# Where the weights of six head pairs are staged in an attention and feed-forward kernel

## The chip, the core and the metric

The kernel runs on one core of one Trainium2 chip. A core has TensorE (PE: matmuls, with PEld for the loads of its stationary operand), VectorE (DVE), ScalarE (ACT), GpSimd (POOL) and SyncE (SP, which here issues nearly all DMAs). The metric is the time of one execution on the device, in microseconds (us): 3020.89 us is the median of three runs of the kernel before, which ranged from 3020.09 to 3022.32 us. Everything is float32. The first dimension of an on-chip tile is the 128 partitions; a tile of `[128, 1024]` float32 takes 4 KB of each partition.

## What is computed

One transformer block over 2048 rows of 1024 columns. Cut to what matters:

```python
q, k, v = (layernorm(x) @ W for W in (Wq, Wk, Wv))     # 16 heads of 64 columns
q, k = rotary(q), rotary(k)
attn = softmax(causal(q @ k.T) / sqrt(64)) @ v          # per head
x = x + layernorm(attn @ Wo)
Wg, Wu, Wd = dequant_nf4(...)                           # 16-value codes times block scales
x = x + layernorm((silu(layernorm(x) @ Wg.T) * (layernorm(x) @ Wu.T)) @ Wd.T)
```

## The kernel before

**Numbers in two parts.** A float32 operand of a matmul is split in a high part (a cast to the type fp32r, on ACT) and a low part (the rest, a subtraction on DVE or POOL). A product is then three matmuls (`mm3`, lines 110 to 115): high by high, high by low, low by high.

**Stages.** The 16 heads are worked on in eight pairs `m = 0..7`, since two heads of 64 columns fill 128 columns of a weight. For a pair, `prep_qkv` (line 221) prepares three weights by `prep_w` (line 174): the 1024 x 128 columns of Wq, Wk and Wv. Then `qkv(m, c)` (line 224) makes the three products for each of four row groups `c` of 512 rows; it applies the rotary table `tab`, splits the results and stores them to DRAM (`qs`, `ks`, `vs`). Attention (`scores`, `weighted`) reads them back by head.

The q, k and v of pairs 0 and 1 are made at the start. Those of pairs 2 to 7 are made beside the attention: while the attention of one pair runs, three or four `(m, c)` groups of later pairs are interleaved with it (lines 384 to 418; `pace` ties each product to a score matmul, so that they spread over 85% of the pair). Line 394 asks for a new pair's weights when the attention of a pair starts; where the new pair begins within an attention pair, `group` (line 379) asks for them. Then follow the output projection, the dequantized gate and up matmuls, and the down projection.

**Preparing a weight.** `prep_w` takes a 4 KB room `wf`, loads 512 KB into it from DRAM on SP's queue (line 177), and makes the two parts in an 8 KB room `w`: two casts on ACT (line 184) and, for pairs from the third on (`m > 1`), two subtractions on DVE (line 186). There are 18 such loads for `m > 1`, three to a pair.

**Rooms.** All SBUF tiles come from tags with a fixed number of rooms:

```python
SLOTS = {"hd": (7, 8), "w": (3, 8), "xc": (4, 8), "pa": (6, 8), "pb": (2, 4), "f4": (4, 4), "pw": (3, 4), "t2": (3, 2), "ol": (1, 2)}
```

The first number is the count of rooms, the second the KB of each. The rooms of a tag are handed out in the order in which the program asks for them, and a load waits until the room it is given is free. During the attention `f4` (four rooms) serves, for each `(m, c)` group, the table `tab`, the split q and k (`hl`, one each) and the split v (`vo`): four requests to a group. In the kernel before it also serves `wf`. `pb` (two rooms) holds the weight Wv of pair 1 in two halves at the start (`prep_qkv(1, ("pa", "pa", "pb"))`, line 346; `prep_w` makes two tiles of four blocks for this tag); it is asked for again only after the attention, for the rows of the output projection (line 504). The `w` tag has three rooms, one for each weight of the pair in work: a new weight can be cast when the last product with the old one in its room is done.

**Order.** The order of each engine's instructions is fixed when the program is built: a planner takes them by the program's order as their priority and by a modelled time line (`schedule_with_timeline_sim=True`, line 830), in which an instruction is placed when its operands and its room are there. At run time each engine goes through its list in order and waits at semaphores. DMAs issued on SP are a list of that kind too.

Of the kernel before, what the change touches and what calls it, by code (L numbers as in the profile page):

```python
# [10 lines left out]
F32 = mybir.dt.float32  # L11
# [13 lines left out]
P = 128  # L25
KE = E // P
# [31 lines left out]
def block_kernel(ctx, tc, x, wq, wk, wv, wo, gu_codes, gu_scales, d_codes, d_scales, cos_sin, out):  # L58
# [15 lines left out]
    def slot(tag, shape, dtype, name):  # L74
        assert int(np.prod(shape[1:])) * 4 <= SLOTS[tag][1] * 1024, (tag, shape)
        return sb.tile(shape, dtype, tag=tag, name=name, bufs=SLOTS[tag][0])
# [25 lines left out]
    def f32(ap):  # L102
        return ap.bitcast(F32)
# [69 lines left out]

    def prep_w(w, m, scale, tag="w"):

        wf = slot("f4", [P, KE, P], F32, "wf")
        load(wf, w[:, m * P : (m + 1) * P].rearrange("(k p) n -> p k n", p=P))
        n = KE // 2 if tag == "pb" else KE
        parts = []
        for k0 in range(0, KE, n):  # L180
            t = slot(tag, [P, 2, n, P], FR, "w")
            for k in range(0, n, STEP):
                src, hi, lo = wf[:, k0 + k : k0 + k + STEP], t[:, 0, k : k + STEP], t[:, 1, k : k + STEP]
                A.activation(hi, src, AF.Copy, scale=scale)  # L184
                if m > 1:
                    V.scalar_tensor_tensor(lo, src, scale, f32(hi), ALU.mult, ALU.subtract)
                else:
                    if scale != 1.0:
                        G.tensor_scalar(src, src, scale, 0.0, ALU.mult, ALU.add)
                    G.tensor_tensor(lo, src, f32(hi), ALU.subtract)  # L190
            parts += [t[:, :, k, :] for k in range(n)]
        return parts
# [28 lines left out]
    def prep_qkv(m, tags=("w", "w", "w")):  # L221
        return [prep_w(w, m, sc, tag) for w, sc, tag in zip((wq, wk, wv), (0.125, 1.0, 1.0), tags)]
# [207 lines left out]
    m = KE - 1  # L430
# [403 lines left out]
```

## Time and profile before

| | us |
|---|---|
| median of three runs | 3020.89 |
| the profiled execution | 3012.18 |
| its span in the profile | 3010.4 |
| PE busy | 2912.1 |
| DVE busy | 2032.5 |
| ACT busy | 1697.9 |
| POOL busy | 954.8 |

The span is the time between the first and the last instruction of the profiled execution; 1.8 us of its time lie outside it. Busy is the time in which an engine had an instruction in work. The granted clock (PEclk) is the share of full speed that TensorE was given; over the whole span it is 0.992. DMA share is the mean busy share of the core's 16 DMA engines. The attention lies roughly between 165 and 1490 us.

### The profile page before, as it was taken

The numbers are of one execution on the slowest core, as the hardware profiler recorded it, in microseconds if no ns is written. First come the engines' busy times: TensorE is split into PE (matmuls) and PEld (weight loads), VectorE is DVE, ScalarE is ACT, GpSimd is POOL, SyncE is SP. The second block draws the span as 40 slices with busy tenths as digits, with TensorE's granted clock in tenths as the row PEclk, the third lists the DMA queues.
The fourth block names the chain that finished last, engine by engine and source line by source line (L and its number), as shares of the span: only waits on it lengthen the run. The fifth ranks groups of instructions, "written<-read, shape, count | busy, mean of one in ns | idle before, by whom it ended". The sixth has DMA issues, their size and how long they took to land.

```text
span 3010.4 us, 42538 instructions
## 1 busy us (share of the span) xinstructions
PE 2912.1 (97%) x14168; PEld 2406.1 (80%) x14168; DVE 2032.5 (68%) x4171; ACT 1697.9 (56%) x3569; POOL 954.8 (32%) x1055
## 2 busy tenths in 40 slices
PE   7989999999998999999999999999999999999998
PEld 6868888787877787777787888888888888888886
DVE  6567778787867677777666667776666677444347
ACT  4256667776766666676565555655555566333234
POOL 5344344443444343454332121222221223100034
PEclk9999999999999999999999999999999999999999
DMA  8787665657557558472356344434434444744446
GB/s 295 271 255 233 213 214 186 213 171 226 157 196 195 172 176 254 139 229 90 123 178 230 109 138 139 154 129 140 135 121 135 139 151 151 255 140 144 150 144 234
DMA packets 271740, 536.01 MB, mean 178 GB/s; under 512 B 22944, under 2 KB 113056, under 8 KB 255648
## 3 DMA queue, kind: packets, MB, share of 16 engines
q1 hardware_dynamic: 269344, 529.10, 54.3%
q10 hardware_dynamic: 2176, 4.19, 0.4%
q8 instruction: 112, 1.84, 0.3%
q14 instruction: 108, 0.88, 0.1%
HBM read 371.98 MB, written 161.22 MB: 177 GB/s over the span
## 4 chain that ended last, share of the span: by engine, by line
PE 79%; DMA 9%; DVE 5%; ACT 2%; issue 1%; POOL 1%; SPq 1%; POOLq 0%; ACTq 0%; DVEq 0%
PE bk L112 14%; PE bk L114 14%; PE bk L113 14%; PE pt L315 6%; PE qkv L112 4%; PE qkv L114 4%; PE qkv L113 4%; PE o L320 3%; PE o L319 3%; PE s L273 3%; PE s L275 3%; PE pj L466 2%; PE pj L464 2%; PE pj L465 2%; DMA wf<-in_wq 2%
## 5 line engine op out<-in xcount | busy, mean ns | idle before, releaser
L305 POOL TENSOR_SCALAR prob<-prob,rc 128x512 f32<-128x512 f32 (+3 forms) x640 | 404.9, 659 | 440.1 <-DVE rc L300 231.0
L112 PE MATMUL bk<-x,wt 128*128 128x512 f32 x1376 | 534.1, 390 | 4.6 <-ACT x L118 3.7
L113 PE MATMUL bk<-x,wt 128*128 128x512 f32 x1376 | 535.9, 389 | 0.0
L114 PE MATMUL bk<-x,wt 128*128 128x512 f32 x1376 | 535.7, 389 | 0.0
L283 ACT ACTIVATE prob<-s,mxs 128x512 f32<-128x512 f32 (+3 forms) x640 | 402.6, 633 | 145.9 <-DVE mxs L281 88.7
L119 DVE TENSOR_TENSOR pw<-pt,pw 128x512 fp32r<-128x512 f32 (+3 forms) x640 | 378.4, 601 | 119.7 <-ACT pw L118 117.9
L529 ACT ACTIVATE ln<-cs,bias 128x512 f32<-128x512 f32 x520 | 359.8, 716 | 107.0 <-DVE mb L535 20.4
L118 ACT CAST pw<-pt 128x512 fp32r<-128x512 f32 (+3 forms) x640 | 324.1, 527 | 169.6 <-PE pt L315 137.0
L315 PE MATMUL pt<-ident,prob 128*128 128x128 f32 x2176 | 345.4, 275 | 7.3 <-DVE pw L119 6.0
L315 PEld LDWEIGHTS pt<-ident,prob 128*128 128x128 f32 x2176 | 267.6, 141 | 62.0 <-issue 7.7
L112 PEld LDWEIGHTS bk<-x,wt 128*128 128x128 f32 x1376 | 258.4, 188 | 59.1 <-ACT x L118 3.9
L114 PEld LDWEIGHTS bk<-x,wt 128*128 128x128 f32 x1376 | 258.7, 188 | 53.9
L113 PEld LDWEIGHTS bk<-x,wt 128*128 128x128 f32 x1376 | 258.8, 188 | 53.5
L281 DVE TENSOR_REDUCE mxs<-s 128x1 f32<-128x512 f32 x384 | 260.9, 681 | 58.6 <-PE s L275 57.3
L273 PE MATMUL s<-k,q 128*128 128x512 f32 (+3 forms) x640 | 265.0, 415 | 23.9 <-ACT prob L283 19.7
L320 PE MATMUL o<-pw,v 128*128 128x512 f32 (+3 forms) x640 | 247.0, 388 | 8.3 <-DVE pw L119 7.6
L319 PE MATMUL o<-pw,v 128*128 128x512 f32 (+3 forms) x640 | 243.8, 381 | 8.6 <-ACT pw L118 6.7
L112 PE MATMUL qkv<-xc,w 128*128 128x512 f32 x576 | 230.9, 401 | 11.8 <-ACT w L184 6.3
L113 PE MATMUL bk<-bt,at 128*128 128x512 f32 x616 | 239.6, 389 | 0.0
L114 PE MATMUL bk<-bt,at 128*128 128x512 f32 x616 | 238.8, 389 | 0.0
L112 PE MATMUL bk<-bt,at 128*128 128x512 f32 x616 | 238.6, 389 | 0.0
L275 PE MATMUL s<-k,q 128*128 128x512 f32 (+3 forms) x640 | 235.6, 371 | 0.0
(150 smaller groups left out, 5504.7 us busy)
## 6 DMA issues: line engine op xcount, KB each, us to landing
xc<-xd SPq DMA_DIRECT2D x96, 1024.0 KB, 9.1
q<-qs SPq DMA_DIRECT2D x128, 256.0 KB, 6.8
ast<-S SPq DMA_DIRECT2D x44, 512.0 KB, 3.7
cs<-in_gu_scales SPq DMA_DIRECT2D x172, 128.0 KB, 3.2
cs<-in_gu_codes SPq DMA_DIRECT2D x86, 256.0 KB, 3.0
A<-in SPq DMA_DIRECT2D x66, 256.0 KB, 2.1
S<-in SPq DMA_DIRECT2D x66, 256.0 KB, 3.1
ast<-A SPq DMA_DIRECT2D x33, 512.0 KB, 4.5
```

Source lines behind the costliest of these rows:

```text
L112: r = T.matmul(o, lhsT=w[:, 0], rhs=xx[:, 0], start=first, stop=False)
L113: T.matmul(o, lhsT=w[:, 0], rhs=xx[:, 1], start=False, stop=False)
L114: T.matmul(o, lhsT=w[:, 1], rhs=xx[:, 0], start=False, stop=last)
L119: return V.tensor_tensor(lo, src, f32(hi), ALU.subtract)
L273: mm = T.matmul(s, lhsT=q[:, 0, j * P : (j + 1) * P], rhs=k[:, b:e], start=True, stop=False)
L275: T.matmul(s, lhsT=q[:, 1, j * P : (j + 1) * P], rhs=k[:, b:e], start=False, stop=True)
L283: A.activation(prob[i][:, j, : e - b], s, AF.Exp, bias=mx, scale=sign, accum_out=sums[:, j % BATCH, i : i + 1])
L305: G.tensor_scalar(p, p, rc[:, jj % BATCH, i : i + 1], 0.0, ALU.mult, ALU.add)
L315: T.transpose(pt[:, j * P : (j + 1) * P], prob[kb // 4][:, j, kb % 4 * P : (kb % 4 + 1) * P], ident)
L319: T.matmul(o[:, cs], lhsT=v[:, kb, :], rhs=pw[:, 0, cs], start=kb == 0, stop=False)
L320: T.matmul(o[:, cs], lhsT=v[:, kb, :], rhs=pw[:, 1, cs], start=False, stop=kb == nk - 1)
L529: A.activation(ln, c8, AF.Prelu, bias=bias_of[ab], scale=ab[0], alpha=ab[2])
```

## The change

One line. The staging room of a weight is taken from `pb` for pairs from the third on (`m > 1`), and from `f4` as before for the first two.

```diff
     def prep_w(w, m, scale, tag="w"):
 
-        wf = slot("f4", [P, KE, P], F32, "wf")
+        wf = slot("pb" if m > 1 else "f4", [P, KE, P], F32, "wf")
         load(wf, w[:, m * P : (m + 1) * P].rearrange("(k p) n -> p k n", p=P))
```

No load, cast, subtraction or matmul is added or taken away. The 18 weights of `m > 1` now share two rooms that nothing else uses during the attention, and the four rooms of `f4` serve `tab`, `hl` and `vo` alone.

## The prediction

> **What bounds the kernel now.** I began with the page. TensorE is busy for all but 98 us of the span, so whatever this change brings has to come out of those 98 us, or out of matmuls that ran at a lower clock.
>
> ```profile
> span 3010.4 us, 42538 instructions
> ...
> PE 2912.1 (97%) x14168; PEld 2406.1 (80%) x14168; DVE 2032.5 (68%) x4171; ACT 1697.9 (56%) x3569; POOL 954.8 (32%) x1055
> ```
>
> Next I asked for everything that touches the tile wf, from 300 us on, where the weights of pairs 3 to 7 are prepared (m = 2 comes earlier). The rows give each load's time in SP's queue (ns, min/median/max), who waited for the loads, and their time to landing.
>
> ```profile
> L177 SPq DMA_DIRECT2D wf<-in_wv x5: 1065/3812/10472, 353.8 to 1147.6; - x5
> ...
>   ACT w L184: 14.1, 6
> ...
> DMA to landing us min/median/max: 6.0/12.3/16.2
> ```
>
> A load lands 12.3 us after its issue, and ACT's list has the cast in it sooner than that: ACT stood still for 14.1 us at six casts. The loads start at 340, 535, 730, 931 and 1145 us. So I cut out the stretch around each (busy us and counts of PE, PEld, DVE, ACT and POOL, then granted clock, DMA share, GB/s):
>
> ```profile
> 336.00:362.00 26.00, 24.70 (x141) 20.28 (x139) 21.74 (x52) 21.10 (x56) 5.47 (x10) 1.00 1.00 332
> 527.00:556.00 29.00, 26.04 (x129) 20.08 (x128) 23.85 (x66) 20.79 (x55) 11.04 (x16) 0.88 0.88 251
> 728.00:752.00 24.00, 21.82 (x115) 16.91 (x114) 18.25 (x47) 17.52 (x45) 5.97 (x10) 1.00 1.02 299
> 930.00:964.00 34.00, 27.53 (x146) 21.34 (x145) 27.78 (x77) 25.95 (x70) 11.80 (x19) 0.95 1.02 286
> 1137.00:1166.00 29.00, 24.73 (x127) 20.39 (x126) 21.48 (x58) 19.58 (x52) 5.65 (x11) 0.88 1.03 285
> ```
>
> and the long stretches between them:
>
> ```profile
> 362.00:527.00 165.00, 163.26 (x901) 136.93 (x899) 127.82 (x325) 113.25 (x296) 77.43 (x104) 1.00 0.58 191
> 556.00:728.00 172.00, 167.64 (x929) 140.91 (x928) 131.18 (x336) 116.46 (x310) 76.33 (x102) 1.00 0.57 181
> 752.00:930.00 178.00, 171.75 (x940) 142.63 (x939) 134.38 (x352) 119.16 (x321) 78.65 (x108) 1.00 0.51 162
> 964.00:1137.00 173.00, 168.36 (x909) 139.66 (x909) 125.08 (x324) 110.86 (x292) 73.91 (x102) 0.99 0.56 179
> ```
>
> In the five windows PE is idle for 142 - 124.8 = 17.2 us (12%), between them for 688 - 671.0 = 17.0 us (2.5%). The DMA engines are full in the windows and half used between them. And three windows have a lower clock.
>
> The waits of the last window show the path, from the load to ACT, to DVE and to PE:
>
> ```profile
> ACT w L184 <- DMA wf<-in_wq: 4.8, 1, 4.8
> ...
> DVE w L186 <- ACT w L184: 4.1, 1, 4.1
> PE qkv L112 <- ACT w L184: 3.9, 1, 3.9
> ```
>
> Two finer stretches price the clock that follows:
>
> ```profile
> 946.80:950.20 3.40, 3.40 (x12) 2.56 (x11) 2.42 (x8) 1.99 (x6) 0.26 (x1) 0.51 1.16 241
> ...
> 1155.00:1162.00 7.00, 5.35 (x14) 4.27 (x15) 4.86 (x10) 6.03 (x15) 2.17 (x4) 0.51 1.00 287
> ```
>
> **The change, part by part.** Nothing is added or removed; what moves is when the 18 loads may be issued.
>
> *Why they are late now.* In f4 the three requests of a new pair come after tab, hl, hl and vo of the previous group, so a load starts only when that group is nearly over: the third pair's first load, at 185.02, was released by POOL's rotary addition (L251), the last reader of that group's tab. In pb a load has only older weights before it. The rooms alternate: q of pair m+1 takes the room of k of pair m, k that of v; v takes the room of its own q. So q and k of the next pair can be issued as soon as this pair's k and v are cast, most of a pair earlier (190 us lie between windows), and v as soon as its q is cast. With the load there, a cast waits only for its w room, so q, k and v are cast one by one behind the last group's three products. At m = 3 those products ended at 314, 327 and 336, against casts at 356 to 361 now: v's load would get some 20 us, more than the longest landing (16.2).
>
> *What the waits cost PE.* By the waits of the windows: m = 3, 0.2 (qkv behind the cast); m = 4, nothing (its 2.1 us gap at 538 follows ACT's wait for a store of at); m = 5, 1.3 + 0.5 (the second, a pw cast queued behind on ACT); m = 6, 2.6 + 1.4 (pw and prob behind two waiting casts) + 1.4 (scores waiting for q<-qs, issued at 953.6, behind weight loads in SP's list and in full DMA engines); m = 7, 3.9. Sum 11.3 us.
>
> *The clock.* PE worked 3.40 us at 0.51 after the gap at m = 6 and 5.35 us at 0.51 around that of m = 7. At full clock it would have saved 3.40 x 0.49 + 5.35 x 0.49 = 1.7 + 2.6 = 4.3 us.
>
> The trace has the half clock after gaps of at most 2.6 us at m = 6. [...]
>
> *What is late next.* 11.3 + 4.3 = 15.6 us would go if nothing else waited. But 11.3 is only two thirds of the windows' 17.2 us of idle: the rest ends on prob, pw and q, and would still do so. I credit two thirds: 15.6 x 2/3 = 10.4 us. Bounds: nothing at all, up to windows as quiet as their neighbours (17.2 - 0.025 x 142 = 13.7) with all three half-clock stretches gone (4.3 + 3.0 for the 5.96 us of PE work between 537 and 544), 21.0 us.
>
> *The third pair.* Its pb rooms are held by pair 1's Wv until the last product of (1, 3) ends at 178.3; q's load then starts about 7 us earlier than now, but in front of the four 1 MB loads of xc (178 to 181). Gain: at most the 0.9 us for which PE waits there. Loss: 1 MB at that window's 314 GB/s is 3.3 us, and a half-clock step like that of 168 to 175 (6.83 us long) 3.4 more. I take zero, nearest to the 0.9.
>
> *Edits at no cost.* f4 now serves four requests per group with four rooms, so each kind gets its own last room back; tab for the next group waits for the rotary of the last, a group (30 us or more) before it is used. The casts moved forward cost ACT 1.2 and DVE 1.4 us each; ACT is 66%, DVE 75% busy between the windows, and that room hides them. If it were not there, three pairs of casts would cost up to 4 us a pair.
>
> *The added wait.* v's load waits on SP for the subtraction (L186) of its q. Behind it on SP stand at and vs stores, tab, and the loads of v and q that the next scores need. It is free if SP comes to it after the cast. Its price otherwise is a rival below.
>
> *The plan itself.* A changed room reorders all that follows. The stretches between windows run from 1.1% idle (362 to 527) to 3.5% (752 to 930); all 688 us at either end would be 9.6 us less or 7.0 us more. I take zero.
>
> [...]
>
> **Forecast.** The profiled execution (3010.4 span + 1.8) lies 8.7 us under the median; I carry the difference over to the median: 3020.9 - 10.4 = 3010.5 us. Its own range is 3000 (21.0 off) to 3015.
>
> **Rivals.** *Same, 3021:* the stalls only move, because the loads are planned little earlier, or because the order of the rest eats the gain (a loss of 7.0, above). For it: DVE and ACT limit these stretches too. Against: 12% of idle here, 2.5% beside.
>
> *Slower, 3029:* SP reaches v's load before DVE has cast q, and is held with the scores' q loads behind it. The price per hold, from m = 6, is 1.4 us of PE wait and 1.7 us of half clock, 3.1; six holds cost 18.6, less 10.4 is +8.2. Beyond three holds it eats the gain. For it: SP's waits for DVE's hl average 7.6 us (213.7 in 28). Against: those 20 us of slack.
>
> **How the numbers follow.** Forecast 0.6, same 0.2, slower 0.2. The range, 3000 to 3029, runs from the far end of the forecast to the slower case and leaves out about 0.17. 0.2% is 6 us, about what a measurement of this kernel can tell from no change; faster by more takes the forecast's 0.6, within it 0.2, slower 0.2.
>
> **What would show it.** Right: wf loads of q and k tens of us before their casts; ACT's 14.1 us behind wf nearly gone; no half clock near m = 6 and 7; PE busy down about 4 us; SP's new wait behind L186 short. Wrong: loads still within 15 us of their casts, casts waiting for v, or new gaps behind q<-qs.

## The result, and the profile after

The changed kernel takes 3040.13 us (median of five runs, 3037.76 to 3043.68) against 3020.89, a ratio of 1.0069 (95% interval 1.0054 to 1.0083). It is slower by about 21 us, where I forecast a gain of 10.4. Its profiled execution is the median one, while that of the kernel before lay 8.7 us below its median: the two spans are 27.9 us apart, the two medians 19.2. The page of the changed kernel:

```profile
span 3038.3 us, 42520 instructions
...
PE 2927.1 (96%) x14168; PEld 2417.4 (80%) x14168; DVE 2035.4 (67%) x4171; ACT 1695.3 (56%) x3569; POOL 958.8 (32%) x1055
```

PE has the same 14168 matmuls and is busy 15.0 us longer with them: within the span its clock was halved for 86.4 us instead of 49.7. The other 12.9 us of the span are more idle time.

Yet the loads moved as described. The tile wf of the changed kernel from 300 us on (loads in SP's queue, who waited, landing):

```profile
L177 SPq DMA_DIRECT2D wf<-in_wv x5: 373/384/392, 327.8 to 1147.5; - x5
L177 SPq DMA_DIRECT2D wf<-in_wq x4: 378/380/498, 343.2 to 953.5; - x4
...
  DVE w L186: 1.5, 2
...
DMA to landing us min/median/max: 3.6/3.9/16.6
```

No cast of ACT waits for a load any more (14.1 us before), and the median load lands in 3.9 us instead of 12.3: eight of the 13 were issued into idle DMA engines (a DMA share of 0.00 to 0.01 in the 2 us before the issue) and landed in 3.6 to 4.0 us, the other five, issued into full ones (0.97 to 1.07), in 8.2 to 16.6. The same five windows, and below them the four stretches between them (busy us and counts by engine, granted clock, DMA share, GB/s):

```profile
336.00:362.00 26.00, 25.65 (x147) 21.48 (x145) 21.18 (x51) 18.87 (x48) 9.95 (x12) 1.00 0.99 310
527.00:556.00 29.00, 26.02 (x128) 20.88 (x128) 21.68 (x61) 19.21 (x56) 9.00 (x13) 0.94 0.72 227
728.00:752.00 24.00, 22.27 (x109) 17.69 (x108) 16.17 (x37) 14.57 (x37) 9.82 (x13) 0.93 0.38 128
930.00:964.00 34.00, 30.80 (x164) 24.70 (x163) 28.39 (x68) 24.43 (x65) 16.85 (x20) 1.00 0.38 128
1137.00:1166.00 29.00, 29.00 (x160) 24.51 (x159) 23.26 (x55) 20.18 (x52) 11.61 (x16) 1.00 0.46 143
```

```profile
362.00:527.00 165.00, 157.08 (x853) 130.82 (x853) 124.32 (x315) 110.00 (x289) 69.47 (x95) 0.99 0.59 186
556.00:728.00 172.00, 162.91 (x882) 133.73 (x881) 127.05 (x329) 111.71 (x297) 72.52 (x104) 0.99 0.61 181
752.00:930.00 178.00, 171.41 (x938) 141.74 (x937) 131.21 (x348) 118.16 (x318) 72.99 (x103) 0.99 0.59 188
964.00:1137.00 173.00, 161.41 (x867) 133.27 (x867) 123.42 (x332) 110.60 (x299) 68.68 (x99) 0.97 0.64 200
```

In the windows PE's idle time fell from 17.2 to 142 - 133.7 = 8.3 us, and the DMA share of the last three from 1.0 to 0.4. Between them it rose from 17.0 to 688 - 652.8 = 35.2 us. The windows are fixed in time, though, while the changed kernel runs up to 30 us later, so they no longer hold the same work; the next count is free of that.

**Where it was lost.** I gave every matmul the median spacing that its kind has in the trace of before, and read when each kernel had done the same amount of matmul work. The kernel before has done 300 us of it at 341.0, 700 us at 769.0 and 1500 us at 1641.6. The changed kernel is 7.8 us late at the first of these marks, 25.1 at the second, 26.5 at the third. So 7.8 us go by the end of the attention of pair 0, nearly all of them in its first 35 us ("start"), 17.3 in the attention of pairs 1, 2 and most of 3 ("middle"), and only 1.4 in the rest, where the windows of m = 6 and 7 lie.

Cut by the same count, the work of the five windows takes the changed kernel 130.4 us instead of 142, and that of the four stretches between them 715.0 instead of 688. The gain of the windows was there, 11.6 us, and more than twice as much was lost between them.

### The profile page after: what moved, and what is told of

Its sections match the earlier page's. It is cut to its first block, busy times and chain, and to the rows that moved or that the text cites. A ratio compares the mean times of both kernels' runs of the same rounds, so it can differ in the third digit from the quotient of the medians.

```text
span 3038.3 us, 42520 instructions
## 1 busy us (share of the span) xinstructions
PE 2927.1 (96%) x14168; PEld 2417.4 (80%) x14168; DVE 2035.4 (67%) x4171; ACT 1695.3 (56%) x3569; POOL 958.8 (32%) x1055
## 4 chain that ended last, share of the span: by engine, by line
PE 79%; DMA 10%; DVE 5%; ACT 3%; issue 2%; POOL 1%; SPq 0%; POOLq 0%; ACTq 0%; DVEq 0%
PE bk L112 14%; PE bk L113 14%; PE bk L114 14%; PE pt L315 5%; PE qkv L112 5%; PE qkv L113 4%; PE qkv L114 4%; PE o L320 3%; PE s L273 3%; DMA xc<-xd 3%; PE o L319 3%; PE s L275 3%; PE pj L464 2%; PE pj L466 2%; PE pj L465 2%
## 5 line engine op out<-in xcount | busy, mean ns | idle before, releaser
L273 PE MATMUL s<-k,q 128*128 128x512 f32 (+3 forms) x640 | 266.7, 418 | 36.3 <-ACT prob L283 27.9
```

Source lines behind the costliest of these rows:

```text
L273: mm = T.matmul(s, lhsT=q[:, 0, j * P : (j + 1) * P], rhs=k[:, b:e], start=True, stop=False)
```

## The experiments

The first reading of the traces gave these theories. START: the third pair's loads, now ahead of x and k, cost the start. HOLD: SP, waiting for L186 with v's load, holds what stands behind it. PLAN: the planner's new order happens to be a worse one. EARLY WORK and EARLY LOADS: what comes earlier (casts and products, or transfers) stands in the way. OL: the single `ol` room, whose store to `at` lands late. All ratios are to the kernel before, on the same chip; where an expectation gives a time, it counts from the 3020.9 us of the kernel before, or from b_x1's 3011 where it says so. The table has each kernel's ratio and, from its one profiled execution, its extra time against the kernel before in the three stretches. One execution is a small sample (on one chip the kernel before took 3010.8 to 3025.2 us), so a few us in one cell say little. The table also has the time at which ACT issued the load of the rotary table `tab` of group (1, 3), with which the start's loss turns out to go.

| kernel | ratio (95%) | tab issued at | start | middle | rest |
|---|---|---|---|---|---|
| before | 1 | 167.6 | 0 | 0 | 0 |
| the change | 1.0069 (1.0054 to 1.0083) | 172.4 | +7.8 | +17.3 | +1.4 |
| from4 | 1.0095 (1.0079 to 1.0112) | 172.4 | +7.5 | +18.6 | +2.6 |
| only3 | 1.0028 (1.0018 to 1.0039) | 172.5 | +10.0 | +2.9 | -4.6 |
| tied | 1.0048 (1.0032 to 1.0063) | 166.6 | -0.3 | +21.7 | -2.1 |
| hold | 0.9997 (0.9986 to 1.0007) | 168.1 | +0.3 | 0.0 | +1.5 |
| late | 1.0034 (1.0022 to 1.0046) | 168.2 | -0.1 | +16.5 | -2.0 |
| b86 | 0.9987 (0.9974 to 1.0000) | 167.1 | -0.8 | +1.2 | +4.2 |
| a86 | 1.0080 (1.0065 to 1.0095) | 173.3 | +7.4 | +15.6 | +3.2 |
| b_x1 | 0.9986 (0.9976 to 0.9995) | 168.2 | +0.3 | +1.1 | -4.3 |
| a_x1 | 1.0012 (1.0003 to 1.0020) | 172.4 | +7.1 | +7.9 | -5.4 |
| from4_x1 | 1.0000 (0.9990 to 1.0010) | 171.7 | +6.7 | +2.1 | -7.1 |
| startheld | 1.0060 (1.0044 to 1.0076) | 168.5 | +2.9 | +19.4 | +2.8 |
| startheld_x1 | 0.9984 (0.9974 to 0.9993) | 167.1 | +1.8 | +5.6 | -3.9 |
| b_off | 1.0023 (1.0012 to 1.0033) | 168.9 | +0.7 | +2.4 | +6.8 |
| from4_off | 1.0031 (1.0019 to 1.0042) | 173.6 | +9.4 | +3.5 | +2.1 |
| a_off | 1.0037 (1.0024 to 1.0050) | 173.3 | +8.0 | +4.1 | -1.9 |
| startheld_off | 1.0024 (1.0014 to 1.0035) | 168.8 | +3.4 | +6.1 | +1.9 |

### The parts of the change

**from4** and **only3** do the change for the pairs from the fourth on, and for the third alone.

```diff
-        wf = slot("pb" if m > 1 else "f4", [P, KE, P], F32, "wf")
+        wf = slot("pb" if m > 2 else "f4", [P, KE, P], F32, "wf")     # from4
+        wf = slot("pb" if m == 2 else "f4", [P, KE, P], F32, "wf")    # only3
```

> The change for pairs from the fourth on (m > 2); the third pair (m = 2) stages its weights in f4 as before. Theory START (the third pair's casts stand in ACT's list too early and block the first scores, about 7 us): 3033. Theory HOLD (the loads' new wait for the subtraction L186 holds SP's list, 76.5 us in total, and late q, at and xc behind it cost PE): most holds remain, so 3034 to 3040. Theory PLAN (any reordering of this program loses, whatever is moved): anywhere from 3020 to 3045, with no link to the place.

> The change for the third pair alone (m == 2). START: 3028, with ACT's wait of 5 us and more on wf near 180 us. HOLD: 3021 to 3024, since only the third pair's third load waits. PLAN: anywhere from 3020 to 3045.

only3 loses 0.28%, as START forecast (3028, or 1.0024), and by its trace all of it at the start. from4 was meant to leave the start alone and didn't: with the third pair in f4, it is the fourth pair's first loads that find pb empty, and its trace has loads of wf at 174.0 and 174.9, ahead of x, as the change has at 172.4 and 175.6. So from4 has both losses; it says nothing against START.

**tied** is from4 with the loads held in SP's list until their cast is near.

```diff
+        ld = load(wf, ...)
+        if m > 2:
+            after(ld, stored["k", m - 1, 3] if w is wv else stored["v", m - 1, 1])   # the SP stores of ks and vs
```

> The change from the fourth pair on, with each load placed in SP's list behind a store that is issued long after the cast it waits for: q and k of pair m behind the v store of group (m - 1, 1), v behind the k store of (m - 1, 3). The loads are still early enough, and SP's wait for L186 should be gone. HOLD with START: 3009 to 3015, below before. START alone: 3033. PLAN: 3030 or more.

The wait that my slower rival named is there in the changed kernel. SP's waits (us in total, times, longest):

```profile
SPq L177 <- DVE w L186: 76.5, 9, 14.6
```

tied has no such wait at all, and no loss at the start, and still loses 0.48%: 21.7 us in the middle. HOLD with START had forecast 3009 to 3015 here. So HOLD is not what costs the middle.

**hold** puts the wait without the rest into the kernel before, by a small store that needs L186.

```diff
             parts += [t[:, :, k, :] for k in range(n)]
+            if m > 2:
+                load(seen[:, m, :], f32(t[:, 1, n - 1, :8]))    # ahead of parts
```

> The kernel before (wf in f4 for all), with one small store on SP (8 columns of the low part, 4 KB) after each weight's subtraction for m > 2: SP's list gets 15 waits for L186 and nothing else of the change. HOLD: 3030 to 3036. START: 3021, the stores being small. PLAN: anywhere from 3020 to 3045.

0.9997, but its SP waited for the subtraction only 2.3 us in all, in three short waits: the planner put the stores where the parts were nearly done. The run made hardly a hold, so it is no evidence on one; only tied is.

**late** keeps Wv in f4, ties the loads of q and k, and ties the casts behind the split of v of (m - 1, 3).

```diff
+        wf = slot("pb" if m > 2 and w is not wv else "f4", [P, KE, P], F32, "wf")
+        if m > 2 and w is not wv: after(ld, stored["v", m - 1, 1])
+                if m > 2: after(cast, stored["cast", m - 1, 3])
```

> From the fourth pair on, q and k are staged in pb with their loads placed early (behind the v store of group (m - 1, 1)), v in f4 as before, and all casts are placed behind the last split of v of group (m - 1, 3), that is where the kernel before has them. So the loads are early and the casts and products are not. Theory EARLY WORK (the casts and products that come sooner put the loads of the next rows and heads, the stores of at and the products out of step): 3008 to 3016, no slower than before, with ACT's wait on wf mostly gone. Theory EARLY LOADS (the loads themselves, ahead in SP's list, cost): 3027 or more, like the tied version. Theory PLAN (any reordering loses): 3025 or more.

1.0034, with 16.5 us lost in the middle, but ACT now waited 16.6 us for Wv's loads. It is not a clean test of early casts. Nor did it hold the products back: counted in matmul work they start as early as in the change (see "The middle").

### Other suspects

**b86** and **a86** set `PACE = 0.86` (0.85) in the kernel before and in the changed one: another order, the same mechanisms.

> The kernel before with its pace at 0.86 instead of 0.85: a small reordering that touches no room and no load. It shows how much a reordering alone moves the time. PLAN: 3022 to 3035. EARLY WORK, EARLY LOADS and OL: 3014 to 3020, the same as before.

> The changed kernel at a pace of 0.86 instead of 0.85, which left the kernel before where it was (0.9987). If the loss belongs to the change and not to one unlucky order: 3030 to 3045. If it is one unlucky order: it may fall to 3020 or rise over 3050.

0.9987 and 1.0080: the loss is still there at the other pace. That speaks against PLAN, but weakly, since the new pace changes the order little: no group's first product moves by more than 2.2 us of matmul work.

**a_olf4** and **b_olpb** give `ol` more rooms: `ol = slot("f4", ...)` in the change, `slot("pb", ...)` in the kernel before.

> The changed kernel with the output tile ol of a head taken from the four rooms of f4 instead of its own single room, so that ACT's copy does not wait for the store of the one before (23 us of ACT's time in the changed kernel, 11.5 before). Theory OL (the single room, with its store late in SP's list, carries most of the loss): 3020 to 3027. Theory PLAN: no link, 3030 to 3050. If the loss comes from xc and q alone: 3036 to 3040.

> The kernel before with ol taken from the two empty rooms of pb instead of its single room (the weights stay in f4). OL: 3005 to 3013, since ACT's 11.5 us behind the store go, with some of the half clock that follows them. PLAN (a tuned order, of which every reordering loses): 3020 or more.

They take 3426.19 us (1.1350, 1.1334 to 1.1366) and 3072.57 us (1.0178, 1.0164 to 1.0192). In b_olpb ACT no longer waits for a store of `at` (11.5 us in six waits before, from 165 to 1370 us), and the kernel is 57 us slower than the kernel before on the same chip: perhaps the one room also kept an order, which no run shows. OL, as a remedy, fell.

### The reload of x

**b_x1** and **a_x1** load x once instead of once per group. All groups then multiply the rows of the first, so the output is not the block's; the runs only show what the reload costs.

```diff
+    once = []
     def load_x(c):
-        tiles = []
+        if once:
+            return once
+        tiles = once
```

> The kernel before without the reloading of x: the four rooms of xc are loaded once (rows of c = 0) and every later group multiplies with them, so that the output is not the reference's; 21 of the 22 reloads of 4 MB beside the attention fall away. All theories: faster than before by some 5 to 20 us, since products no longer wait for x; it is the reference for the next run.

> The changed kernel with the same thing left out (x loaded once). Theory BACKLOG (with the weights' loads gone from the pair's boundary, the full DMA queue now holds up the loads of x, tab and q and the stores of at instead, which engines wait for): without the 4 MB per group there is no backlog to fight over, the gain that was predicted appears except for the start, and this is 5 to 15 us below b_x1 after 300 us of the span, 0 to 10 below in all. Theory EARLY WORK (the earlier casts and products themselves crowd ACT and DVE): 8 to 20 us above b_x1. Theory PLAN: no link.

b_x1 gained 0.14%, less than the 5 us expected at the least. The two were run together: 3010.95 and 3019.49, 8.5 us apart instead of the change's 19.2. That is against BACKLOG, which expected a_x1 below b_x1, and within what EARLY WORK expected. By the stretches, a_x1 loses 6.8 us to b_x1 at the start and 6.8 in the middle (the change: 7.8 and 17.3): without the reload more than half of the middle's loss goes, and the start's stays.

**from4_off** spreads the products over 10 to 85% of a pair's scores in from4.

```diff
-                want = PACE * (3 * i + n) / (3 * len(now)) * anchors[-1][0]
+                want = (0.1 + 0.75 * (3 * i + n) / (3 * len(now))) * anchors[-1][0]
```

> The change from the fourth pair on, with the products of each attention pair spread over 10% to 85% of it instead of 0% to 85%, so that the first product of a pair comes about as late as the weights let it in the kernel before. BACKLOG (the loads of x then no longer meet those of the next heads' k and v): 3012 to 3022. EARLY WORK: 3015 to 3025, since casts are still early but products are not. PLAN: 3035 or more.

It recovers two thirds of from4's loss (1.0095 to 1.0031), less than BACKLOG and EARLY WORK expected and more than PLAN did: the middle falls from 18.6 to 3.5 us, the start stays.

### Start and middle apart

For the next runs START+X says that the start and the reload of x carry everything. **from4_x1** is from4 with x loaded once. **startheld** is the change with the third pair's loads and casts held back; **startheld_x1** adds x loaded once.

```diff
+        if m == 2:
+            after(ld, stored["v", m - 1, 3])        # SP: behind the store of vs of (1, 3)
...
+                if m == 2:
+                    after(cast, stored["cast", m - 1, 3])   # ACT: behind the cast of that v
```

> The weights of pairs 3 to 7 in pb, those of the third in f4, and x loaded once instead of once per group (its output is not the reference's; to be set beside b_x1, 3011). START+X: the third pair and the reload of x carry the whole loss, so nothing is lost here: 3011, or up to 10 less, since the waits for late weights (9.7 us in b_x1) go. PLAN: the order of each plan decides, and the result lies anywhere between 3000 and 3030, above 3016 as likely as not.

> The change, with the third pair's loads held in SP's list behind the store of v of (1, 3), and its casts in ACT's list behind the split of that v, so that they no longer stand ahead of the exponentials of the first head. START+X: the 8.5 us of the start go and the reload of x stays: 3031, 1.0035 of the kernel before. EARLY CASTS (the casts ahead of the exponentials are the whole start loss): the same, and no PE gap above 2 us between 165 and 195. PLAN: anywhere from 1.000 to 1.010.

> startheld with x loaded once (its output is not the reference's; to be set beside b_x1, 3011, and a_x1, 3019.5). START+X: equal to b_x1, 3011, or up to 10 less. If the start's loss is not the casts' place but the loads' contention with x and k: as a_x1, 3019. PLAN: anywhere between 3000 and 3030.

startheld_x1 equals b_x1 (0.9984, 0.9986), as START+X forecast: here the change costs nothing in all, and brings nothing. from4_x1 lies 0.14% (4 us) above b_x1; against b_x1 it loses 6.4 us at the start and 1.0 in the middle. startheld came out at 1.0060, not at the expected 1.0035: the start fell to 2.9 us, but the middle grew to 19.4. The two losses don't simply add up between plans.

**The start.** ACT's timeline of the kernel before and of the changed one (start us, us, what, idle time before it and what ended that):

```profile
167.62 0.55 ACTq L227 DMA_DIRECT2D tab<-in_cos_sin  x1
168.21 0.37 ACT L283 ACTIVATE prob<-s,mxs 128x128 f32<-128x128 f32 x1 [0.93 <-DVE sh L248]
```

```profile
172.39 0.55 ACTq L227 DMA_DIRECT2D tab<-in_cos_sin  x1
172.99 0.37 ACT L283 ACTIVATE prob<-s,mxs 128x128 f32<-128x128 f32 x1 [5.21 <-DMA k<-ks]
...
182.71 1.15 ACT L184 ACTIVATE w<-wf 128x512 fp32r<-128x512 f32 x2 [5.62 <-DMA wf<-in_wq]
```

ACT issues this one table itself, and was idle for 5.2 us around that issue, until a load of k landed that the table has nothing to do with; PE then waited 5.4 us for the exponentials behind it. The trace has the semaphore by which each DMA reports its landing. In the traces of the kernel before and of the change there are eight; for 1407 and 1405 of 1426 issues the last DMA on the same semaphore is the eighth before, and none of the 1426 comes before that DMA has landed. The table's issue shares its semaphore with a load of q in the kernel before, which landed at 167.54, and with k's second part in the changed one, which was issued at 162.60 and landed at 172.31. In both, ACT's list waits for that semaphore just ahead of the issue, which came 0.08 us after the landing. In the seven other kernels of the table with the issue at 171.7 or later, the profile names a load of k for ACT's idle time there too, 5.6 to 6.3 us.

The table above carries this through all kernels: where the issue comes at 171.7 or later, the start loses 6.7 to 10.0 us; where it comes by 168.9, at most 3.4. So it looks as if not the bytes of the weights cost the start, but which earlier DMA the table's issue was paired with. Second, a cast waited 5.6 us for its early load, ahead of the exponentials in ACT's list; how much that adds is not shown, and from4, without this wait, loses as much. No run changed the semaphore alone.

**The middle.** Waits for DMAs on ACT and PE in the middle stretch (us in total, times, longest), of the kernel before, the change, tied, a_x1 and from4_off, in this order:

```profile
ACT w L184 <- DMA wf<-in_wq: 4.9, 3, 2.9
ACT ol L322 <- DMA at<-ol: 4.5, 2, 2.4
PE qkv L112 <- DMA xc<-xd: 1.3, 1, 1.3
```

```profile
ACT ol L322 <- DMA at<-ol: 15.5, 5, 4.6
...
PE qkv L112 <- DMA xc<-xd: 6.0, 5, 3.6
```

```profile
ACT ol L326 <- DMA at<-ol: 20.8, 6, 6.8
...
PE qkv L112 <- DMA xc<-xd: 8.5, 5, 3.5
```

```profile
ACT ol L326 <- DMA at<-ol: 3.8, 2, 2.0
```

```profile
ACT ol L322 <- DMA at<-ol: 0.8, 1, 0.8
PE qkv L112 <- DMA xc<-xd: 0.7, 1, 0.7
```

The wait for weights has gone, and two others stand in its place: products that wait for x, and ACT's copy to `ol`, which waits for the store of the last one. What brought them is, by the runs, where the products stand. Counted in matmul work, the first product of m = 3 starts at 313.5 us before and at 303.3 in the change (303.3 in tied, 304.5 in startheld), and that of m = 4 at 491.7 and 483.4. The order of a list is fixed, so this is the planner's doing: the weights' lateness had held these products back, and without it those of m = 3, 4 and 7 start 8 to 10 us of work sooner and those of m = 5 5.5 (m = 6: no change). There x has only the four rooms that the previous group's last product frees, so its 4 MB are issued just before: at m = 4 the last part of x landed 6.7 us ahead of the first product in the kernel before, and 0.2 us behind its start in the change. The five stores of `at` that ACT waited for landed after 7.4 to 13.8 us (the mean of all in the stretch is 7.7). In only3, whose later weights are late as before, m = 3 starts at 314.2 and the middle loses 2.9 us.

Early products alone cost little: in b_x1 they start as soon as in the change (305.2 and 484.4), and without the reload of x its middle loses 1.1 us. In late they start at 304.5 and 483.1 with the reload, and it loses 16.5, though its late Wv has a part in that. Nor is it the early loads of weights by themselves: from4_off issues those of m = 4 among x's (343.8 and 349.9) as the change does (343.2 and 348.5), and loses 3.5 us. But the spread doesn't put the products back all the way: in from4_off m = 3 starts at 306.1, m = 4 at 490.3. And which of the two waits carries the loss is open; a86, with as large a loss, waits 16.1 us for stores and only 2.3 for x.

### Both undone

The last runs put the spread of from4_off on the kernel before (**b_off**), on the change (**a_off**) and on startheld (**startheld_off**). EARLY PRODUCTS is the reading just given.

> The kernel before, with its products tied to 10 to 85% of a pair's scores instead of 0 to 85%. EARLY PRODUCTS (late weights already hold the first products back in the kernel before, so the spread changes little): 0.998 to 1.002. PACE (the spread is a better pace for any kernel): 0.995 or less, and then from4_off recovered nothing that belongs to the change.

> The change, with products tied to 10 to 85%. EARLY PRODUCTS: only the start is lost, as in from4_off: 1.002 to 1.004, and no wait for x above 1 us between 341 and 795. PLAN (each plan its own accident): anywhere from 1.000 to 1.010.

> startheld with products tied to 10 to 85%: both suspected losses removed, the early weights kept. EARLY PRODUCTS + START: nothing is lost, and what is left of the predicted gain shows: 0.996 to 1.001. If a third loss is left: 1.003 or more, as from4_off.

The spread itself costs 0.23%, which I had not expected; perhaps because a pair's products lie closer together in it (75 instead of 85% of the scores). Against b_off the change now costs 1.0037 / 1.0023, 0.14%, no product of a_off waits for x in the middle, as EARLY PRODUCTS had it, and its middle is within 2 us of b_off's. The start's loss stays (7.3 us more than b_off), and the rest gives 8.7 us back. startheld_off, without most of the start's loss, equals b_off. Its middle is 3.7 us above that of b_off and its rest 4.9 below. None of the kernels with early weights beats its counterpart with late ones beyond the intervals.

## Why the prediction was wrong

**The mechanism of the loads: right.** q and k of the next pair were loaded long before their casts, and ACT's 14.1 us went. Cut by matmul work, the window of m = 7 lost its half clock and its 4.3 us of idle time fell to 0.2. That of m = 6 kept both, for another reason (below). The eight loads that now find idle engines land in 3.6 to 4.0 us, where the median of before, in full ones, was 12.3.

**"What is late next": wrong.** I credited two thirds of 15.6 us because the other third of the idle time ended on prob, pw and q. Of the windows alone it came true, partly perhaps because other work moved: by matmul work they are 11.6 us shorter. But I let the stretches between them stay as they were, and they took 27.0 us more. Even with most of the start's and the middle's loss undone nothing is left of the credit: startheld_x1 and b_x1 are within 0.1% of each other, as are startheld_off and b_off (the last two by work: windows 16.6 us shorter, stretches between 11.8 longer). In the last two, from 165 to 1370 us, ACT and PE wait for DMAs of wf, at, x and q as follows: b_off 17.6 + 4.0 + 2.4 + 1.7 = 25.7 us, startheld_off 2.0 + 9.1 + 7.8 + 4.4 = 23.3 us. I looked for what was late next within the windows of before. I didn't ask what would be late next once the products came earlier. At m = 6 it is the load of q that the next scores need, where the profile of the changed kernel has this wait, and half clock in this stretch around its end:

```profile
PE s L273 <- DMA q<-qs: 6.1, 1, 6.1
```

```profile
985.80:992.60 6.80, 3.11 (x8) 2.58 (x9) 2.20 (x10) 0.67 (x3) 0.00 (x0) 0.50 1.06 237
```

**"Edits at no cost" and "the plan itself": wrong, and the largest miss.** I counted the casts that move forward (1.2 and 1.4 us) and not the products that move with them. The waiting weights were also a brake on the order, and with the brake gone the middle lost 17.3 us. That is more than the 7.0 that I gave a worse plan, which I had measured on stretches of the old order. from4, tied, startheld and a86, other orders with the same early products, lose 15.6 to 21.7 us there.

**"The third pair": wrong by its size and its cause.** I took zero between -0.9 and +6.7. The start lost 7.8 us in the change, and only3, with this part alone, 7.4 in all. I had priced 1 MB in front of x; the longest stall was ACT's in front of its own table issue.

**"The added wait": wrong as a forecast, and yet not the cause.** I called it free; SP waited 76.5 us in nine times. The rival's price of 3.1 us per hold would make that 28 us. tied has none of it and loses as much in the middle. So the rival "slower, 3029" had the sign, not the reason, and by a chance of 0.2.

**The clock: wrong in sign.** Instead of 4.3 us saved, 36.7 us more were run at half clock, at most 18.4 us of lost matmul time, against 15.0 us of longer busy time. In the change PE ran at half clock from 880.0 to 883.4 after a gap of 2.2 us, shorter than the 2.6 us gap at m = 6 before.

**What stays open:** why a_x1, startheld_x1 and startheld_off keep 4 to 7 us in the middle over their counterparts; what the semaphore and the early cast each cost at the start; and what HOLD costs by itself, since no run made the hold alone.

## What to carry over

A transfer that is late may be what keeps the work behind it in place. Before taking such a wait away, list what the planner will move forward with it, and where the other loads of that moment (here x, k, q and a store with one room) would then have to be. And look at what a moved DMA does to the issues behind it: here one table's issue came to wait for another load than before.

## What the runs showed of the hardware

- In the traces of the kernel before and of the change none of 1426 DMAs was issued, on SP's list or ACT's, before the last one on its semaphore had landed, the eighth before it for 1407 and 1405 of them, whatever that carried: ACT was idle for 5.2 to 6.9 us at the issue of its table in the nine kernels where the profile names the load of k there, and 0.9 us in the kernel before.
- More rooms cost time here: two rooms instead of one for `ol` made the kernel before 1.8% slower; `ol` in the four shared rooms of f4 put the change 13.5% above it.
- Eight loads of 512 KB on SP's queue, issued into idle DMA engines in the change (a DMA share of 0.00 to 0.01 in the 2 us before), landed in 3.6 to 4.0 us; the 15 of the kernel before from 300 us on, into full ones (0.92 to 1.25), in 12.3 (median).
- Half clock came, but for the last stretch, at the span's end, in eight stretches before (four of 3.41 us, four of 6.83) and 15 in the change (ten of 3.41, three of 6.83, one of 10.24, one of 13.65); with the last 86.4 us in place of 49.7.
